# Last layer of a four-layer convolution kernel: two 64-column matmuls side by side, two kinds of tap pairs, weights prepared ahead by GpSimd

## The chip, the core and the metric

The kernel runs on one core of one Trainium2 chip. Its metric is device time in microseconds (us), the median over the timed executions. A core has a matmul engine (TensorE, "PE", whose weight loads are listed as "PEld"), VectorE ("DVE"), ScalarE ("ACT"), GpSimd ("POOL") and SyncE ("SP"), which here only issues DMAs. Each engine has an instruction stream of its own; they meet at semaphores.

## The reference, cut to what matters

Four layers are applied to `x` of 2 x 128 channels x 128 x 128 in float32: an attention along columns, four directional scans, a deformable convolution, and the layer that is changed. Before each stands a group normalisation.

```python
x = x + _L3_conv_ref(_gn(x), L3_conv_weight, L3_conv_bias)

def _L3_conv_ref(x, weight, bias):      # KERNEL 4, STRIDE 2, padding 1
    patches = _extract_patches(x)       # b c h w p q: 64 x 64 patches of 4 x 4
    hmt1 = jnp.einsum('up,bchwpq,qv->bchwuv', _H, patches, _H)
    hmt2 = jnp.einsum('pu,bchwpq,qv->bchwuv', _H2, patches, _H2)
    m1 = jnp.einsum('bchwuv,ocuv->bohwuv', hmt1, weight[:half])
    m2 = jnp.einsum('bchwuv,ocuv->bohwuv', hmt2, weight[half:])
    o1 = jnp.einsum('au,bohwuv,cv->bohwac', _IH, m1, _IH)
    o2 = jnp.einsum('au,bohwuv,cv->bohwac', _IH2, m2, _IH2)
    hmult = jnp.concatenate([o1, o2], axis=1)
    ...
    return out + bias
```

`_H` and `_H2` hold only 1 and -1, `_IH` and `_IH2` only 1/4 and -1/4. Each patch gives a 2 x 2 block of outputs; the lower 64 output planes use one set of matrices, the upper 64 another. The scan layer before it matters for one reason: a row of it is a 9-tap convolution of the finished row before, so 4 x 127 steps follow one another strictly.

## The kernel before, in words

The image stays in SBUF as `res` (128 channels on the partitions). `layer0_prepare`, `layer0_attention`, `Merge.run`, `layer1` (the scans), `layer2` and `layer3` run one after the other. A helper, `InOrder`, keeps the instructions of an engine in the order of the Python program; all of them show under line 81.

`layer3` (line 1652) works in 32 blocks: for each of two images, 16 blocks of `RB = 8` rows, which are 4 x 64 patches. Per block:

- `normalise` (ACT, two activations of 128 x 640) writes the normalised even and odd columns, with a rim of zeros that GpSimd sets, to `col0` and `col1`.
- `transform` (DVE, eight `tensor_tensor` of 128 x 640) makes four planes `x` from sums and differences of neighbouring columns: the transform along a row is done, that down the column is not.
- `multiply` (PE) does 32 matmuls, each with 128 x 128 weights out of `weff` and 256 moving columns: for each of the four planes and both output rows, four taps summed in PSUM. One float32 matmul is two instructions in the trace, with a weight load each.
- `finish` (ACT two, DVE eight operations) combines the four planes, adds the bias and the residual `res`, and SP stores the block.

`multiply` of block i stands ahead of `finish` of block i-1 and `transform` of block i+1, and all tiles but one are double. The weights `weff` are made between the layers: `w3` (1 MB) is loaded once layer 2 is over, DVE makes sums and differences of it (lines 1673 and 1674), and DVE and ACT scale 32 pieces each (lines 1682 and 1686).

`layer1` (line 1039) starts with a group norm, loads the weights of three scans on ACT's DMA queue (`wl`, line 1033), lets GpSimd add taps (`ws`, line 1035), and normalises four rows on ACT before the first step of the scan:

```python
        ahead = 4
        for h in range(ahead):
            normalise(h)
```

`load_columns` fetches tiles `x1t` that only the fourth scan reads; three of these loads are issued at the start of the layer.

Three other places of the kernel use matmuls with fewer than 128 output columns, which lie side by side on PSUM's partitions: `ps_off` (line 1234, layer 2, four outputs of 32), and in `layer0_prepare` `ps_m` and `pg` (two of 64).

Of the kernel before, what the change touches and what calls it, by code (L numbers as in the profile page):

```python
# [7 lines left out]
F32 = mybir.dt.float32  # L8
I32 = mybir.dt.int32
AF = mybir.ActivationFunctionType  # L10
ALU = mybir.AluOpType
# [5 lines left out]
N = 2  # L17
# [1011 lines left out]
def scan_weights(env, prm, pool, d):  # L1029

    nc = env.nc
    wl = pool.tile([P, 9, P], F32, name=f"wl{d}", tag=f"wl{d}")
    nc.scalar.dma_start(out=wl, in_=prm["wscan"][:, d])
    ws = pool.tile([P, 4, P], F32, name=f"ws{d}", tag=f"ws{d}")
    nc.gpsimd.tensor_tensor(ws, wl[:, 2:9:2, :], wl[:, 1:8:2, :], ALU.add)
    return wl, ws


def layer1(env, prm, res, both, x1_d, st_gn, st_next, first):

# [3 lines left out]
    with ExitStack() as ctx:  # L1046
# [3 lines left out]
            gs, gb = env.group_norm(cp, pn, st_gn, "l1")  # L1050
        pp = ctx.enter_context(tc.tile_pool(name="l1ps", bufs=2, space=PSUM))
        weights = [first] + [scan_weights(env, prm, cp, d) for d in range(1, 4)]


        lines = [
# [10 lines left out]
        CB = 8  # L1066

        def load_columns(w0):
            t = sp.tile([P, N, CB, S], F32, name="x1t", tag="x1t")
            nc.sync.dma_start(out=t, in_=x1_d[:, :, w0 : w0 + CB, :])  # L1070
            return t

# [576 lines left out]

def layer3(env, prm, res, st_gn, out):

    nc, tc = env.nc, env.tc
    flip = (1, 0, 2, 3)
    RB = 8
    with ExitStack() as ctx:  # L1660
        cp = ctx.enter_context(tc.tile_pool(name="l3c", bufs=1))
        bias = cp.tile([P, 1], F32, name="bias3", tag="bias3")
        nc.scalar.dma_start(out=bias, in_=prm["b3"])
        weff = cp.tile([P, 4, 2, 4, P], F32, name="weff", tag="weff")
        with tc.tile_pool(name="l3w", bufs=1) as wp:
            ta = wp.tile([P, 16 * P], F32, name="ta", tag="ta")
            tb = wp.tile([P, 16 * P], F32, name="tb", tag="tb")
            nc.scalar.dma_start(out=ta, in_=prm["w3"])
            a, b = ta, tb
            for bit in range(2):  # L1670
                va = a.rearrange("p (h t k) -> p h t k", t=2, k=P << bit)
                vb = b.rearrange("p (h t k) -> p h t k", t=2, k=P << bit)
                nc.vector.tensor_tensor(vb[:, :, 0], va[:, :, 0], va[:, :, 1], ALU.add)
                nc.vector.tensor_tensor(vb[:, :, 1], va[:, :, 0], va[:, :, 1], ALU.subtract)
                a, b = b, a
            what = a.rearrange("p (u v o) -> p u v o", u=4, v=4)
            for u in range(4):
                for c in range(2):
                    for q in range(4):
                        to = weff[:, u, c, q, :]  # L1680
                        sign = (1, -1, 1, -1)[u]
                        nc.vector.tensor_scalar(
                            to[:, 0:64], what[:, u, (c + 1) ^ q, 0:64], sign / 16, None, ALU.mult
                        )
                        sign = (-1, 1, 1, -1)[u] * (-1, 1)[c]
                        nc.scalar.mul(  # L1686
                            to[:, 64:128],
                            what[:, (0, 3, 2, 1)[u], (3, 2)[c] ^ flip[q], 64:128],
                            sign / 16,
                        )  # L1690

        sp = ctx.enter_context(tc.tile_pool(name="l3s", bufs=2))
        with tc.tile_pool(name="l3pn", bufs=1, space=PSUM) as pn:
            gs, gb = env.group_norm(cp, pn, st_gn, "l3")
        pp = ctx.enter_context(tc.tile_pool(name="l3ps", bufs=2, space=PSUM))
        pe, dve, act = (InOrder(tc, e) for e in (nc.tensor, nc.vector, nc.scalar))
        blocks = [(n, h) for n in range(N) for h in range(0, S, RB)]

        def normalise(i):

            n, h = blocks[i]
            lo, hi = max(0, h - 1), min(S, h + RB + 1)
            cols = [
                sp.tile([P, RB + 2, 65], F32, name=f"col{k}", tag=f"col{k}") for k in range(2)
            ]
            nc.gpsimd.memset(cols[0][:, :, 0:1], 0.0)  # L1706
            nc.gpsimd.memset(cols[1][:, :, 64:65], 0.0)  # L1707
            for k in range(2):
                if h == 0:
                    nc.gpsimd.memset(cols[k][:, 0, :], 0.0)  # L1710
                if h == S - RB:
                    nc.gpsimd.memset(cols[k][:, RB + 1, :], 0.0)
            rows = slice(lo - h + 1, hi - h + 1)
            for k in range(2):
                act.activation(
                    cols[k][:, rows, 1 - k : 65 - k],
                    res[n][:, lo:hi, 1 - k :: 2],
                    AF.Identity,
                    bias=gb[:, n : n + 1],
                    scale=gs[:, n : n + 1],  # L1720
                )
            return cols

        def transform(cols):

            x = sp.tile([P, 4, RB + 2, 64], F32, name="x3", tag="x3")
            t = sp.tile([P, 2, RB + 2, 64], F32, name="t3", tag="t3", bufs=1)
            for k, op in ((0, ALU.add), (2, ALU.subtract)):
                even, odd = x[:, k], t[:, k // 2]
                dve.tensor_tensor(even, cols[0][:, :, 0:64], cols[0][:, :, 1:65], op)  # L1730
                dve.tensor_tensor(odd, cols[1][:, :, 0:64], cols[1][:, :, 1:65], op)
                dve.tensor_tensor(x[:, k + 1], even, odd, ALU.subtract)
                dve.tensor_tensor(even, even, odd, ALU.add)
            return x

        def multiply(x):
            got = []
            for u in range(4):
                ps = pp.tile([P, 2, RB // 2, 64], F32, name=f"m{u}", tag=f"m{u}")
                for c in range(2):  # L1740
                    for q in range(4):
                        pe.matmul(
                            ps[:, c],
                            lhsT=weff[:, u, c, q, :],
                            rhs=x[:, u, q : q + RB - 1 : 2, :],
                            start=(q == 0),
                            stop=(q == 3),
                        )
                got.append(ps.rearrange("p c h w -> p (c h w)"))
            return got  # L1750

        def finish(i, m):

            n, h = blocks[i]
            t = sp.tile([P, 512], F32, name="t", tag="t")
            s = sp.tile([P, 512], F32, name="s", tag="s")
            act.activation(t, m[3], AF.Identity, bias=bias)
            act.copy(s, m[2])
            for half, k in ((slice(0, 64), (0, 1)), (slice(64, 128), (1, 0))):
                dve.tensor_tensor(t[half], m[k[0]][half], t[half], ALU.add)  # L1760
                dve.tensor_tensor(s[half], m[k[1]][half], s[half], ALU.add)
            ot = sp.tile([P, RB, S], F32, name="ot", tag="ot")
            o = ot.rearrange("p (h a) (w c) -> p a c h w", a=2, c=2)
            r = res[n][:, h : h + RB, :].rearrange("p (h a) (w c) -> p a c h w", a=2, c=2)
            tv = t.rearrange("p (c h w) -> p c h w", c=2, w=64)
            sv = s.rearrange("p (c h w) -> p c h w", c=2, w=64)
            for a, op in enumerate((ALU.add, ALU.subtract)):
                dve.tensor_tensor(o[:, a], tv, sv, op)
                dve.tensor_tensor(o[:, a], o[:, a], r[:, a], ALU.add)
            nc.sync.dma_start(out=out[n, :, h : h + RB, :], in_=ot)  # L1770

        count = len(blocks)
        cols = {0: normalise(0), 1: normalise(1)}
        xs = {0: transform(cols.pop(0))}
        ms = {}
        for i in range(count + 1):
            if i < count:
                ms[i] = multiply(xs.pop(i))
            if i >= 1:
                finish(i - 1, ms.pop(i - 1))  # L1780
            if i + 2 < count:
                cols[i + 2] = normalise(i + 2)
            if i + 1 < count:
                xs[i + 1] = transform(cols.pop(i + 1))

# [3 lines left out]
def program(ctx, tc, prm, out):  # L1791
# [12 lines left out]
        "sv": dram.tile([P, N, NC, WC, S], F32, name="sv_d", tag="sv_d"),  # L1804
        "sve": dram.tile([P, N, NC, S, WC], F32, name="sve_d", tag="sve_d"),
    }
    x1_d = dram.tile([P, N, S, S], F32, name="x1_d", tag="x1_d")
    mem["px"] = dram.tile([N, TP, TP, P], F32, name="px_d", tag="px_d")
    mem["off"] = dram.tile([N, NT, P, 4, 27], F32, name="off_d", tag="off_d")
# [14 lines left out]
    with tc.tile_pool(name="l1w", bufs=1) as wp:  # L1824
        first = scan_weights(env, prm, wp, 0)
        merge.run(prm, res, mv, st_gn[1])
        merging.close()
        layer1(env, prm, res, both, x1_d, st_gn[1], st_gn[0], first)
    layer2(env, prm, res, mem, tables, st_gn[0], st_gn[1])
    layer3(env, prm, res, st_gn[1], out)  # L1830


def constants(np):
# [126 lines left out]
```

## Time and profile before

| | us |
|---|---|
| median of 3 runs | 5750.13 (5746.08 to 5760.94) |
| the profiled execution | 5755.18 |
| its span, first to last instruction | 5753.0 |
| layer 3's matmuls, first to last | 5298.2 to 5742.6 |
| PE busy in the span | 5381.7 |

The span is cut by time: layer 0's preparation up to about 460, the attention to about 1985, the merge to 2169, the scans to about 3810, layer 2 to 5280, layer 3 from there. In a group's line, the number after the bar is the time in which at least one instruction of the group ran; then the mean length of one, which for matmuls contains the way through the array and so is longer than their spacing.

### The profile page before, as it was taken

The numbers are of one execution on the slowest core, as the hardware profiler recorded it, in microseconds if no ns is written. First come the engines' busy times: TensorE is split into PE (matmuls) and PEld (weight loads), VectorE is DVE, ScalarE is ACT, GpSimd is POOL, SyncE is SP. The second block draws the span as 40 slices with busy tenths as digits, with TensorE's granted clock in tenths as the row PEclk, the third lists the DMA queues.
The fourth block names the chain that finished last, engine by engine and source line by source line (L and its number), as shares of the span: only waits on it lengthen the run. The fifth ranks groups of instructions, "written<-read, shape, count | busy, mean of one in ns | idle before, by whom it ended". The sixth has DMA issues, their size and how long they took to land. (4 is left out here: it accounts for less than half of the span.)

```text
span 5753.0 us, 162512 instructions
## 1 busy us (share of the span) xinstructions
PE 5381.7 (94%) x67323; PEld 4838.1 (84%) x67323; DVE 3775.1 (66%) x7289; ACT 2647.0 (46%) x7928; POOL 1288.8 (22%) x983
## 2 busy tenths in 40 slices
PE   8997999999999708999999999997999999998999
PEld 8866888888888608999999999963999999998888
DVE  3645888888888765555555566643666666666887
ACT  1046989898888774442223320022333333333221
POOL 2113666666666530000000013310000000000000
PEclk9998999999999859999999999998999999999999
DMA  3243333333333491000000001125766677663001
GB/s 146 96 189 105 62 62 60 59 62 62 59 59 58 125 373 50 2 1 1 1 1 1 1 16 39 44 65 118 87 88 88 87 84 90 88 87 50 41 37 41
DMA packets 413668, 401.01 MB, mean 70 GB/s; under 512 B 63488, under 2 KB 368512, under 8 KB 402304
## 3 DMA queue, kind: packets, MB, share of 16 engines
q1 hardware_dynamic: 403856, 363.87, 30.9%
q10 hardware_dynamic: 9072, 26.64, 1.2%
q8 instruction: 541, 8.86, 0.7%
q14 instruction: 199, 1.63, 0.1%
HBM read 251.00 MB, written 139.37 MB: 68 GB/s over the span
## 5 line engine op out<-in xcount | busy, mean ns | idle before, releaser
L81 PE MATMUL pl<-ln,wl 128*128 128x128 f32 (+1 forms) x10160 | 1240.7, 276 | 7.4 <-DVE ln L81 7.2
L81 PEld LDWEIGHTS pl<-ln,wl 128*128 128x128 f32 x10160 | 1176.2, 190 | 18.3 <-DVE ln L81 4.4
L81 ACT ACTIVATE e<-e,mx 128x128 f32<-128x128 f32 x2048 | 793.4, 395 | 0.8 <-DVE mx L81 0.8
L81 ACT COPY sm<-ps_s 128x432 f32<-128x432 f32 (+1 forms) x768 | 318.3, 487 | 803.3 <-PE ps_s L81 803.3
L81 ACT COPY res<-ln 128x128 f32<-128x128 f32 x762 | 262.0, 344 | 720.4 <-DVE ln L81 720.4
L81 POOL TENSOR_TENSOR e<-e,total 128x1024 f32<-128x1024 f32 x256 | 485.9, 1898 | 478.1 <-DVE total L81 470.3
L81 DVE COPY s<-ps_w 100x1152 f32<-100x1152 f32 x256 | 346.5, 1354 | 307.1 <-PE ps_w L81 307.1
L81 PE MATMUL ps_s<-s,xw 100*128 100x144 f32 x4096 | 545.1, 286 | 0.2 <-ACT sm L81 0.2
L81 PE MATMUL po<-sm,wdef 128*128 128x256 f32 x2304 | 539.1, 379 | 0.0
L81 PE MATMUL pl<-ln,ws 128*128 128x128 f32 x4064 | 536.8, 273 | 0.0
L81 POOL COPY et<-et 128x1024 f32<-128x1024 f32 x256 | 516.1, 2016 | 35.7 <-DVE et L81 27.0
L81 PEld LDWEIGHTS ps_s<-s,xw 100*128 100x128 f32 x4096 | 517.1, 190 | 0.7 <-ACT sm L81 0.7
L81 DVE TENSOR_TENSOR v<-pl,c 128x128 f32<-128x128 f32 x508 | 148.2, 292 | 538.0 <-PE pl L81 538.0
L81 PEld LDWEIGHTS pl<-ln,ws 128*128 128x128 f32 x4064 | 494.5, 190 | 0.0
L81 ACT ACTIVATE r<-gen,alphas 128x1536 f32<-128x1536 f32 x256 | 394.9, 1543 | 174.2 <-PE gen L81 145.3
L81 POOL TENSOR_TENSOR res<-ln,x1t 128x128 f32<-128x128 f32 x256 | 134.4, 525 | 1485.1 <-DVE ln L81 1485.1
L81 PEld LDWEIGHTS po<-sm,wdef 128*128 128x128 f32 x2304 | 419.8, 190 | 47.6
L81 PE MATMUL m<-x,weff 128*128 128x256 f32 x2048 | 444.4, 380 | 14.8 <-DVE x L81 14.8
L81 PEld LDWEIGHTS m<-x,weff 128*128 128x128 f32 x2048 | 390.6, 191 | 68.3 <-issue 14.9
L1706 POOL MEMSET col<- 128x10 f32 x32 | 3.7, 116 | 1869.1 <-ACT weff L1686 1490.7
L81 ACT ACTIVATION_READ_ACCUMULATOR e<-e,mx 128x1 f32 x2048 | 396.7, 194 | 0.0
L81 DVE SCALAR_TENSOR_TENSOR ln<-v,res 128x128 f32<-128x128 f32 x1016 | 343.7, 338 | 49.2 <-DVE v L81 1.3
(225 smaller groups left out, 8806.6 us busy)
## 6 DMA issues: line engine op xcount, KB each, us to landing
xw<-px_d SPq DMA_DIRECT2D x1280, 80.0 KB
xa<-in_x SPq DMA_DIRECT2D x16, 1024.0 KB
v_d<-vs SPq DMA_DIRECT2D x16, 1024.0 KB
qb_d<-sb SPq DMA_DIRECT2D x16, 1024.0 KB
qa_d<-sa SPq DMA_DIRECT2D x8, 2048.0 KB
zz<-qb_d SPq DMA_DIRECT2D x1024, 16.0 KB
vt<-v_d SPq DMA_DIRECT2D x64, 256.0 KB
qk<-qa_d SPq DMA_DIRECT2D x256, 64.0 KB
```

Source lines behind the costliest of these rows:

```text
L81: return lambda *a, **k: self.tc.keep_in_program_order(issue(*a, **k))
L1706: nc.gpsimd.memset(cols[0][:, :, 0:1], 0.0)
```

## The change

The 2 x 2 outputs of a patch are sums and differences of PSUM results; the change takes another factoring. Outputs' lower 64 planes ("half 0") and upper 64 ("half 1") now get their own moving operands, so a matmul has 64 output columns, and the two of a pair write partitions 0 to 63 and 64 to 127 of the same PSUM tile `m3`. A block has 48 such matmuls (32 for `m3`'s second half, 16 for its first), hence 96 instructions with float32's two passes, where 64 with 128 columns stood before. Half 0's operands come from pairs of taps across columns (`first`, DVE: `dm`, `dp`, then four `q`), half 1's from pairs across columns and rows (`second`, GpSimd: `ap`, `am`, two `b`). `normalise` writes the odd columns a second time, to a PSUM tile `odd3` (`again`). `combine` (ACT one, DVE four operations) makes the output, and GpSimd adds the residual in `finish`. Tiles `col0`, `col1`, `am`, `dp`, `odd3` are single, `dm`, `ap`, `b`, `ot` double, `q` sixfold, `m3` threefold. The factor 1/16 goes into the group norm's scale.

The weights are made by GpSimd in `layer3_weights`, called at the start of `layer1`: load `ta`, 25 additions and subtractions of 128 x 256, store as `w3_d` (1.3 MB) to DRAM. `layer3` loads them again on SP's queue. `x1t` moves to a pool of its own, opened after that. In the instruction order of the changed kernel, ACT's stream at this place reads: load `wl` of the last scan, load `ta`, store `w3_d` with a wait for GpSimd, the first normalised rows of the scan. GpSimd's reads: a memset, three `ws`, the 25 operations, and nothing more until the fourth scan.

```diff
 def layer1(...):
         weights = [first] + [scan_weights(env, prm, cp, d) for d in range(1, 4)]
+        prepare()
+        xp = ctx.enter_context(tc.tile_pool(name="l1x", bufs=3))
...
-            t = sp.tile([P, N, CB, S], F32, name="x1t", tag="x1t")
+            t = xp.tile([P, N, CB, S], F32, name="x1t", tag="x1t")
...
+def layer3_weights(env, prm, w3_d):
...
+        nc.scalar.dma_start(out=ta.rearrange("p u v o -> p (u v o)"), in_=prm["w3"])
+        pool = nc.gpsimd
...
+                    pool.tensor_tensor(to, ta[:, :, x, part], ta[:, :, y, part], op)
...
+        nc.scalar.dma_start(out=w3_d, in_=w3)
...
 def layer3(...):
-        weff = cp.tile([P, 4, 2, 4, P], F32, name="weff", tag="weff")
...
+        w3 = cp.tile([P, W3], F32, name="w3", tag="w3")
+        nc.sync.dma_start(out=w3, in_=w3_d)
...
+            for t in (gs, gb):
+                nc.vector.tensor_scalar(t, t, 1.0 / 16, None, ALU.mult)
...
+            again = pp.tile([P, 1024], F32, name="odd3", tag="odd3")
+            again = again[:, 0 : (RB + 2) * 65].rearrange("p (h w) -> p h w", w=65)
+            act.copy(again, cols[1])
...
+        def second(cols):
+            even, odd = cols
...
+            pool.tensor_tensor(ap, even, odd, ALU.add)
+            pool.tensor_tensor(am, even, odd, ALU.subtract)
+            for k, op in enumerate((ALU.subtract, ALU.add)):
+                pool.tensor_tensor(b[:, k], am[:, 0::2, :], am[:, 1::2, :], op)
...
+        def first(cols, again):
...
+            for to, op in ((dm, ALU.subtract), (dp, ALU.add)):
+                dve.tensor_tensor(to[:, 0], again[:, :, 0:H], even[:, :, 1:65], op)
+                dve.tensor_tensor(to[:, 1], even[:, :, 0:H], again[:, :, 1:65], op)
+            for k in range(4):
+                q = sp.tile([P, 2, RH, H], F32, name="q3", tag="q3", bufs=6)
...
+                dve.tensor_tensor(q, dp[:, :, lo : lo + RB - 1 : 2, :],
+                    dp[:, :, hi : hi + RB - 1 : 2, :], ...)
...
-            for u in range(4):
-                for c in range(2):
-                    for q in range(4):
-                        pe.matmul(ps[:, c], lhsT=weff[:, u, c, q, :],
-                            rhs=x[:, u, q : q + RB - 1 : 2, :], ...)
+            parts = ((0, one), (1, two))
+            for c in range(2):
+                for q in range(4):
+                    for y in range(2):
+                        for half, part in parts:
+                            if half == 0:
+                                rhs = dm[:, y, q : q + RB - 1 : 2, :]
+                            else:
+                                rhs = ap[:, q : q + RB - 1 : 2, y : y + H]
+                            pe.matmul(ps[part, 1, c], lhsT=rows_weight(half, c, q, y), rhs=rhs, ...)
+            for r in range(2):
+                for x in range(2):
+                    for y in range(2):
+                        for half, part in parts:
...
+                            pe.matmul(ps[part, 0, r], lhsT=ws[:, 2 * r + x, y, part], rhs=rhs, ...)
...
+        def combine(ps):
+            act.activation(c, ps[:, 0, 0], AF.Identity, bias=bias)
...
+                dve.tensor_tensor(g[:, k], c, ps[:, 0, 1], op)
...
+                dve.tensor_tensor(o[:, k], g, ps[:, 1], op)
...
+            pool.tensor_tensor(ot, ot, res[n][:, h : h + RB, :], ALU.add)
             nc.sync.dma_start(out=out[n, :, h : h + RB, :], in_=ot)
...
+        for i in range(-1, count + 2):
+            if i in planes:
+                ms[i] = multiply(*planes.pop(i))
+            if i + 1 < count:
+                planes[i + 1] = second(there[0]) + first(*there)
+            if i - 2 in ots:
+                finish(i - 2, ots.pop(i - 2))
+            if i - 1 in ms:
+                ots[i - 1] = combine(ms.pop(i - 1))
+            if i + 2 < count:
+                there = normalise(i + 2)
```

## The prediction, made before the changed kernel was run

> **What bounds the kernel now.** I read the page first, then the busy time in stretches, then the timeline where the change touches it.
>
> ```profile
> span 5753.0 us, 162512 instructions
> PE 5381.7 (94%) x67323; PEld 4838.1 (84%) x67323; DVE 3775.1 (66%) x7289; ACT 2647.0 (46%) x7928; POOL 1288.8 (22%) x983
> ...
> L81 PE MATMUL m<-x,weff 128*128 128x256 f32 x2048 | 444.4, 380 | 14.8 <-DVE x L81 14.8
> ```
>
> PE is busy nearly everywhere, but that is an average over stages. The stretches of the last layer (us, then busy time and instructions by engine, granted clock, DMA):
>
> ```profile
> core 0: us, PE busy (x) PEld busy (x) DVE busy (x) ACT busy (x) POOL busy (x), PEclk, DMA share, GB/s
> ...
> 5280.00:5298.00 18.00, 0.56 (x2) 0.50 (x2) 14.80 (x52) 9.72 (x38) 0.42 (x6) 0.56 0.17 59
> 5298.00:5745.00 447.00, 444.42 (x2048) 390.58 (x2048) 361.28 (x503) 89.15 (x124) 7.91 (x66) 0.99 0.09 37
> ```
>
> In the 444 us of matmuls PE never rests, DVE has 361 us, GpSimd almost nothing. So this stretch is PE's: one block per 13.815 us (ACT's first read of a finished block is at 5314.42, that of the last at 5742.68, 31 blocks later), 64 instructions at 215.9 ns. Before it PE stands for 18 us while weights are made and the first planes formed. After the last matmul (5742.6) 10.4 us of combining and storing follow.
>
> The second place is the scan's start, where the weights' preparation is put (start, length, engine, instruction):
>
> ```profile
> 2169.11 0.82 ACTq L1033 DMA_DIRECT2D wl<-in_wscan  x2
> ...
> 2173.28 1.26 POOL L1035 TENSOR_TENSOR ws<-wl 128x512 f32<-128x512 f32 x1 [11.26 <-DVE gs_l L44]
> 2173.32 0.20 ACT L45 ACTIVATE gs_l<-gs_l 128x2 f32<-128x2 f32 x1 [6.96 <-DVE gs_l L44]
> 2173.33 0.34 ACTq L1033 DMA_DIRECT2D wl<-in_wscan  x1
> ...
> 2174.59 4.72 ACT L81 ACTIVATE res<-res,gb_l,gs_l 128x128 f32<-128x128 f32 x12 [1.07 <-DVE gb_l L69]
> ```
>
> The third `wl` load waits for nothing of its own, yet is issued 4 us after the other two, behind the activation that waited for DVE: ACT's DMA issues and activations are one line. The scan's first matmul is at 2175.88, right after the first rows of `res`; from there everything is serial, so a delay of these rows is a delay of the end.
>
> **Part 1, the matmuls.** 96 instructions take the place of 64. Alone each would take the same 216 ns (256 columns; fewer weight columns do not shorten the moving stream), so all hangs on whether the two halves run at once. The trace has two such groups:
>
> ```profile
> 384.10 1.09 PE L81 MATMUL pg<-zt 128*64 128x65 f32 x30
> ...
> 3829.47 3.62 PE L1234 MATMUL ps_off<-gx,woff 128*32 128x512 f32 x32
> ```
>
> `pg` has two neighbours of 64 columns: single starts are 384.208, 384.215, 384.267, 384.273, so two every 58.5 ns. 65 columns alone would take 65 x 215.9/256 = 55 ns each: a pair costs one plus 3.5 ns. `ps_off` starts four of 512 every 428 ns, where one alone takes 432. So a pair of 256 is 216 to 219; I take 217. Per block 48 x 217 = 10.42 us, times 32 = 333.3, against 32 x 13.815 = 442.1: **-108.8 us**. Each half reads its own moving tile in `pg` and `ps_off` too.
>
> Against this stands the Trainium skill, "TensorE: Matmul & The Clock Gate", section "Measured speedup vs the span model": three column tiles gave 2.38 times, not 3. At that efficiency (0.79) a pair would take 216 x 2/1.59 = 272 ns, a block 13.05 us, and the gain would be 25 us, about what part 3 takes back. That figure is for single packs with their way through the array; here packs follow one another as in `ps_off`, which measured 3.98 of 4 in steady state. The trace decides.
>
> **Part 2, does anything else need over 10.42 us a block?** DVE: `dm`, `dp` four at 0.82 (row `x<-col`, 818 ns), `q` four at 0.69 (512 elements as `ot<-t,s`, 689), `g` two at 0.42 (256 elements with PSUM as `vs<-ps_zb`, 415), `o` two at 0.69: 8.26 us, less than the 12 of before. ACT: two normalisations 0.93, the copy to PSUM, not in the trace (between the 0.49 of `sm` at 432 elements and 0.97; I take 0.75), bias 0.45: 3.1 us. GpSimd is new here. Its rows for two different inputs (`acc`: 130 elements 467 ns, 260 elements 738) give 0.2 us + 2.08 ns per element: `ap`, `am` 1.55 each, `b` 0.88 twice, `ot` 2.33, two memsets 0.12: 7.4 us. Planes for block i+1 are made while block i multiplies, and most inputs have two buffers, so each queue only has to keep the period.
>
> DVE and GpSimd can stop one another. In the merge:
>
> ```profile
> 2123.76 1.23 DVE L81 TENSOR_TENSOR res<-te,res 128x1024 f32<-128x1024 f32 x1
> 2123.81 3.42 POOL L81 TENSOR_TENSOR res<-te,res 128x1024 f32<-128x1024 f32 x1 [5.25 <-DVE te L81]
> ```
>
> Shortest, median and longest of the same kinds, by tile:
>
> ```profile
> L81 POOL TENSOR_TENSOR e<-e,total x256: 1896/1898/1902, 505.2 to 1979.4; 128x1024 f32<-128x1024 f32 x128
> ...
> L81 POOL TENSOR_TENSOR res<-te,res x16: 2359/3422/3447, 2012.6 to 2158.6; 128x1024 f32<-128x1024 f32 x16
> ```
>
> GpSimd's addition takes 2.36 us without company and 3.42 when it starts inside DVE's: it waits for DVE's end (2124.99), then runs 2.24. In the attention, with DVE at work all the time on operands of which at most one is in SBUF, 256 additions stay within 6 ns of each other. This is what the skill states ("SBUF — State Buffer", section "Who interferes with whom"): a DVE instruction with two SBUF inputs and a GpSimd instruction that reads SBUF exclude one another; with one it does not. `dm`, `dp`, `g`, `o` have one input in PSUM, so only the `q` exclude. By the rule: GpSimd 7.2 + `q` 2.76 = 9.9 us of exclusive time per block, still under 10.42; if every DVE instruction excluded, 7.2 + 8.26 = 15.4, over 13.8. I take the first: no cost. The cover is thin: 0.5 us on the shared entrance, 2.2 on DVE.
>
> **Head and tail of layer 3.** The weights come by DMA (1.3 MB; `ta`'s 1 MB took 4.4 us from 5280.69), before the scales are ready: without the weight operations between them, DVE's chain ends near 5285.2 (5284.6, then 0.15 for `gb` and 0.17 twice for the factor). Normalise 2 x 0.86, copy 0.75, `dm` 0.82: the first matmul at about 5289.0 instead of 5298.2: **-9.2**. `b` and `q` have the 6.9 us of the row matmuls for cover. Both starts pay about 2.2 us of half clock (granted 0.5 until 5302.55). Tail: 0.2 + bias 0.45 + 0.1 + `g` 0.84 + `o` 1.38 + 0.1 + `ot` 2.33 + issue and landing as before 4.2 = 9.6 instead of 10.4: **-0.8**.
>
> **Part 3, the weights at the scan's start.** ACT now has to load `ta` and issue the store of `w3_d` before the first normalised row, and that store waits for GpSimd's 25 operations. Queued behind it: the 12 activations, then DVE's copies, PE's first row, all of the scan. GpSimd: `ta` is issued near 2173.7, behind the third `wl` (0.59 MB). Before, that `wl` landed at 2182.2 because three `x1t` loads (3 MB) were in front; these now wait for the preparation's memory, so `ta` lands earlier: 4.4 us for itself plus 1.4 for `wl`, about 2179.5 (bounds 2177.5 and 2182). The three `ws` (1.27) fit before. Then 25 x 0.73 (256 elements between the rows of 130 and 260; lower bound 0.65 from `L183`, 1.75 ns per element, upper 0.78) = 18.4: 2197.9, issue 0.6, first row at 2198.6 instead of 2174.59: **+24.0** (18 to 29). Nothing hides it, PE has been idle for 173 us there. GpSimd's operations themselves would be free beside the scan; the wait in ACT's line is what costs. The store's bytes and the later `x1t` loads delay nobody: `x1t` is read 1200 us later. SP gets one more issue, at the layer's start, ahead of stores that come 20 us later.
>
> **Sum.** -108.8 - 9.2 - 0.8 + 24.0 = -94.8 on the profiled execution's 5755.2: 5660.4. The median of the runs is 5.05 below that execution, so 5655.
>
> **The rivals.**
> (a) The shared entrance or DVE sets the period. If GpSimd runs at its slow rows (2160 elements in 4780 ns: `ap` 1.63, `b` 0.92, `ot` 2.46) exclusive time is 10.3, and with DVE's in-order queue held at each `q` a period of 11.2 is likely: +25, 5680; at worst (each `q` behind a GpSimd instruction) 11.7, 5697. For it: two queues in strict order. Against: GpSimd's wait overlaps 0.12 of its own start.
> (b) ACT does not stand behind the store (it is handed over and waits elsewhere): +24 goes, 5631. Against: the third `wl`.
> (c) Slower than before: the pairs do not overlap, 96 x 215.9 = 20.73 us a block, +221 - 10 + 24: 5985. The turning point is a pair of 279 ns (32 x 48 x pair = 442.1 + 10 - 24). For it: another pattern than `pg`'s, with 256 columns and weights that change with each instruction. Against: `pg` and `ps_off`. At the skill's packing figure it would end at 5739, not told apart from no change.
>
> **How the numbers follow.** 0.65 for the forecast, 0.19 for (a), 0.09 for (b), 0.03 for (c), 0.01 for the packing in between, 0.03 for slower otherwise or much faster. A measurement here tells about 0.3% (17 us) from no change; all cases but (c), the packing figure and 0.01 of the rest lie beyond that on the fast side: faster 0.95, same 0.01, slower 0.04. The range: part 3's bounds (-6, +5) and a pair at 216 to 219 (-2, +3) give 5647 to 5664 alone; taking in (a) and most of (b), 5634 to 5697.
>
> **What would show it.** Right: `m3`'s matmuls 3072 in about 335 us, starting two together; DVE idle before `dm` or `g`, not PE before `m3`; the first `res` activation near 2198 with a GpSimd release; scan steps as long as before. Wrong: PE idle before `m3` with `q` or `b` as releaser (a); the first row at 2175 (b); 660 us of `m3` (c).

## The result, and the profile after

The changed kernel takes 5645.36 us (median of 4 runs, 5644.19 to 5656.64), the kernel before beside it 5748.1 us (4 runs, 5744.51 to 5760.94). The ratio is 0.9822, with a 95% interval of 0.9802 to 0.9842: 1.8% faster. The forecast was 5655, ten microseconds above. The profiled execution took 5645.21 us, with a span of 5643.4.

From the page of the kernel after, the span and the busy time by engine:

```profile
span 5643.4 us, 164496 instructions
PE 5270.7 (93%) x68347; PEld 4712.5 (84%) x68347; DVE 3697.0 (66%) x7127; ACT 2648.5 (47%) x7896; POOL 1549.2 (27%) x1169
```

There are 1024 more matmul instructions, and PE is still busy 93% of the time: the page alone does not tell what happened. The stretches do (the head of the last layer, then its matmuls; us, then busy time and instructions by engine, granted clock, DMA share, GB/s):

```profile
core 0: us, PE busy (x) PEld busy (x) DVE busy (x) ACT busy (x) POOL busy (x), PEclk, DMA share, GB/s
5280.00:5298.30 18.30, 9.68 (x52) 8.41 (x50) 5.84 (x17) 5.84 (x10) 1.91 (x5) 0.83 0.21 72
5298.30:5634.40 336.10, 335.99 (x3072) 264.45 (x3072) 295.63 (x379) 94.80 (x124) 245.94 (x227) 0.99 0.13 50
```

The last layer's matmuls took 444.42 us for 2048 instructions; now 3072 take 335.99. PE is busy throughout; GpSimd has gone from 8 to 246 us in this stretch, and DVE from 361 to 296. The groups of matmuls, with the idle time of PE before each in the last column, say that nothing was waited for:

```profile
L81 PE MATMUL m<-ap,w 128*64 128x256 f32 x1021 | 229.0, 381 | 0.0
L81 PE MATMUL m<-dm,w 128*64 128x256 f32 x1021 | 228.1, 382 | 0.0
L81 PE MATMUL m<-q,w 128*64 128x256 f32 x512 | 116.1, 380 | 0.0
L81 PE MATMUL m<-b,w 128*64 128x256 f32 x512 | 115.9, 378 | 0.0
```

The busy times of the four groups add up to 689 us in 336: two ran at any time. (The 380 ns are the recorded length of one, from entering to leaving the array; one enters every 216.) The starts of the first `dm` matmul of each block are 12.35 us apart at first, then ten times 10.36, then 10.43 and 10.44 in turn: 215.8 and 217.4 ns for each of 48 pairs.

The other place is the scan's start (start, length, engine, line, instruction, idle time before it and releaser):

```profile
2167.21 0.20 ACT L45 ACTIVATE gs_l<-gs_l 128x2 f32<-128x2 f32 x1 [6.96 <-DVE gs_l L44]
2167.22 0.33 ACTq L1033 DMA_DIRECT2D wl<-in_wscan  x1
2167.89 0.33 ACTq L1681 DMA_DIRECT2D ta<-in_w  x1
...
2174.07 4.81 POOL L1703 TENSOR_TENSOR tb<-ta 128x256 f32<-128x256 f32 x7 [1.48 <-DMA ta<-in_w]
...
2191.29 0.33 ACTq L1720 DMA_DIRECT2D w_d<-w3w  x1
2191.67 4.72 ACT L81 ACTIVATE res<-res,gb_l,gs_l 128x128 f32<-128x128 f32 x12 [24.25 <-POOL w3w L1692]
```

ACT stands for 24.25 us between the scales and the first normalised row, and what released it is GpSimd's last operation on `w3w`, by way of the store that is issued 0.4 us ahead of the row. Before, the row came 1.27 us after the activation of the scales (2173.32 to 2174.59); now 24.46 us after it (2167.21 to 2191.67).

### The profile page after: what moved, and what is told of

Same layout as the page of the kernel before. It is cut to its first block, busy times and chain, and to the rows that moved or that the text cites. A ratio compares the mean times of both kernels' runs of the same rounds, so it can differ in the third digit from the quotient of the medians.

```text
span 5643.4 us, 164496 instructions
## 1 busy us (share of the span) xinstructions
PE 5270.7 (93%) x68347; PEld 4712.5 (84%) x68347; DVE 3697.0 (66%) x7127; ACT 2648.5 (47%) x7896; POOL 1549.2 (27%) x1169
## 5 line engine op out<-in xcount | busy, mean ns | idle before, releaser
L81 PE MATMUL te<-cst_main,e 128*128 128x128 f32 x2048 | 338.5, 288 | 24.5 <-POOL e L81 17.3
L81 DVE COPY et<-te 128x512 f32<-128x512 f32 x512 | 348.1, 680 | 11.5 <-PE te L81 10.9
```

What stands on the lines that cost most here:

```text
L81: return lambda *a, **k: self.tc.keep_in_program_order(issue(*a, **k))
```

## The experiments

Theory: the gain is the pairs of matmuls (108 us) and the shorter head (10 us); all that is paid is ACT's line, held by the store. Rivals: the preparation costs something else; PE's pairing hangs on the order of the instructions or doesn't; DVE and GpSimd are near to being the bound. The kernel before took 5745 us beside the first four runs, 5764 beside the next four and 5754 beside the last two, so what is compared below is mostly stages of the profiles, which repeat far better than whole times. Experiments 4 to 10 are one execution each.

**1. The store issued by SyncE.**

```diff
-        nc.scalar.dma_start(out=w3_d, in_=w3)
+        nc.sync.dma_start(out=w3_d, in_=w3)
```

> The changed kernel with one word changed: the store of w3_d is issued by SyncE instead of ScalarE. Theory (ScalarE's line, held by a store that waits for GpSimd's 25 operations, is all that the preparation costs): the 24.25 us of idle time before the first normalised row go, that row starts within 2 us of the end of the merge's scales, and the kernel runs about 23 us less than the changed kernel's 5645, so near 5622; ratio to the kernel before about 0.978. Rival 1 (GpSimd's work beside the scan costs as well: it excludes VectorE and delays the scan's first steps, or its memory does): 5 to 20 of the 23 us come back as longer first scan steps, 5627 to 5642. Rival 2 (the first row waits for something else of the new part, the load of ta or the third wl): no change, 5645. The loads of x1t, now queued on SyncE behind the store, are read 1200 us later and should cost nothing under any theory.

Measured: 5626.44 us (median of 5), ratio to the kernel before 0.98 (0.9786 to 0.9814); the changed kernel run beside it 5649.34 (median of 4), its ratio to the kernel before 0.9837 (0.9822 to 0.9852). So 22.9 us faster than the changed kernel. The profile at the scan's start:

```profile
2170.80 0.20 ACT L45 ACTIVATE gs_l<-gs_l 128x2 f32<-128x2 f32 x1 [8.05 <-DVE gs_l L44]
2172.11 4.72 ACT L81 ACTIVATE res<-res,gb_l,gs_l 128x128 f32<-128x128 f32 x12 [1.10 <-DVE gb_l L69]
...
2190.49 0.72 POOL L1692 TENSOR_TENSOR tk<-zero,tk 128x256 f32<-128x256 f32 x1
2190.57 0.79 DVE L81 SCALAR_TENSOR_TENSOR ln<-v,res 128x128 f32<-128x128 f32 x1
2191.18 0.77 POOL L1716 TENSOR_TENSOR w3w<-tk 128x256 f32<-128x256 f32 x1
```

The row comes 1.31 us after the scales, as before the change, and GpSimd now prepares the weights while the scan runs. The last three lines are the small remainder of rival 1: DVE's `ln<-v,res`, two inputs in SBUF, starts inside GpSimd's operation and takes 0.79 us instead of its usual 0.29, and GpSimd's next one starts only near its end. Added over the steps beside the preparation this is 2.9 us, and the scan's first pass is 404.0 us long instead of 401.0. The theory holds; the sum from the profile is 23.2 won and 3 paid, 20.2 net, where the medians differ by 22.9 and the runs of the two spread over 16 and 11 us. This is the fastest version of the study.

**2. The preparation alone, with the last layer of before.** The diff to the kernel before is the changed `layer1` and `layer3_weights`; `layer3` stays, and the stored weights are read by nobody.

> The last layer is that of the kernel before (it makes its own weights again), and only the preparation and its store on ScalarE are put in at the scan's start; the stored weights are read by nobody. Theory: the scan's first row comes 23 to 24 us later and all else is as before, so 5748 + 23 = about 5771, ratio 1.004. Rival (the preparation's 24 us are partly won back behind it, as the changed kernel's shorter second layer start suggests, because the program up to the last layer is the same here): second layer's start is 7 us shorter than in the kernel before, about 5764. If the 13 us that the changed kernel gained outside the scan's start and the last layer are only the spread between executions, this profile and the copy of the kernel before show merge ends anywhere from 2153 to 2160 us and layer 2 starts (end of the offsets' matmuls to the first ps_w) anywhere from 35 to 40 us, in no order.

Measured: 5770.22 us against 5744.93, ratio 1.0042 (1.0027 to 1.0058): 25 us slower, on the expected 23. The wait is the same:

```profile
2195.72 4.72 ACT L81 ACTIVATE res<-res,gb_l,gs_l 128x128 f32<-128x128 f32 x12 [24.06 <-POOL w3w L1692]
```

From the scales to the row it is 24.26 us, then matmuls of 444.32 us as in the kernel before. Nothing is won back behind it.

**3 and 4. Both kernels once more.** The changed kernel's first profile was 13.7 us faster than the change accounts for (below). No edit.

> The changed kernel once more, for the spread of its stages between executions: 5645 within 6 us. Theory of spread: the stages up to the scan, and from the last scan step to the first ps_w, differ from the first profile by some us; what the change reaches does not: 3072 matmuls of the last layer in 336.0 us within 0.5, 8.1 us ahead of them, 9.0 behind, 24.2 us of idle time before the first normalised row. Rival (those stages are changed by the change): they repeat within 1 us.

> The kernel before once more, one execution: 5748 within 8 us. Theory of spread: the merge's end and the second layer's start differ from the first profile by up to 7 us while the scan's four passes and the last layer (444.4 us of matmuls) repeat within 1 us. Rival: they repeat within 1 us, and the changed kernel's 13 us there belong to the change.

Measured, by stage, in us (M: end of the merge's last `res` on DVE; G: from the last offsets' matmul of layer 2 to its first `ps_w`; S: from the scales to the scan's first row; H: from the group norm that follows layer 2, at DVE's first `mv_l`, to the last layer's first matmul; L: its matmuls; T: from the last matmul to the end of the span):

| kernel | M | G | S | H | L | T |
|---|---|---|---|---|---|---|
| before, first profile | 2159.8 | 39.4 | 1.27 | 17.74 | 444.42 | 10.45 |
| before_again | 2158.0 | 34.2 | 1.30 | 17.77 | 444.61 | 10.45 |
| preparation_only | 2157.9 | 40.7 | 24.26 | 17.75 | 444.32 | 10.03 |
| changed, first profile | 2153.7 | 35.1 | 24.46 | 8.10 | 335.99 | 9.04 |
| changed_again | 2153.9 | 34.5 | 24.49 | 8.10 | 335.65 | 9.04 |
| store_on_sync | 2156.2 | 34.3 | 1.30 | 7.89 | 336.77 | 9.04 |

S, H, L and T repeat within 0.5 us where the same code runs (but L of store_on_sync is 0.8 to 1.1 us above the other two). G took 39.4 us in one profile of the kernel before and 34.2 in the other (34.2 to 40.7 over the twelve profiles of this study), and M lies anywhere between 2148.4 and 2159.8 in the twelve. The two changed profiles repeated M within 0.2 us, as the rival said, but the later runs, the same up to there in all but the last layer, had 2152.7, 2155.7, 2149.3, 2156.7, 2148.4 and 2157.9. So of the 13.7 us, 10.4 lie in two stages that vary like this from one profile to the next (6.1 in M, 4.3 in G), and the first profile of the kernel before had both near their long end; the rest lies in small differences of the stages between, 1.6 us of it in layer 2's offsets. What makes the two stages vary the runs don't show. The medians of the runs made here side by side, 5744.93 (9 runs) and 5649.34 (4), differ by 95.6 us, within 1 us of the sum of the steps (96.3, below).

**5 and 6. How far apart may the two halves stand?** Each call of `pe.matmul` is two instructions (3072 instructions are 48 calls for each of 32 blocks), so even the changed kernel issues A A B B. The two runs put two calls of a half together, and then a whole accumulation group (8 calls of the columns' part, 4 of the rest).

```diff
-                    for y in range(2):
-                        for half, part in parts:
+                    for half, part in parts:
+                        for y in range(2):
```

```diff
-                for q in range(4):
-                    for y in range(2):
-                        for half, part in parts:
+                for half, part in parts:
+                    for q in range(4):
+                        for y in range(2):
```

(and the same for the loops of `qs` and `b`.)

> The changed kernel with two loops of the matmuls exchanged: two calls of one half (four instructions, since each call of fp32 is two) stand before two calls of the other, instead of one and one. Same 96 instructions per block, same data. Theory (PE starts instructions in order; one starts when its own columns are free and its predecessor has started): A A A A B B B B takes 6 slots for 8 instructions instead of 4, since only the last of a run has the first of the next beside it; 72 slots of 216 ns, 15.55 us per block instead of 10.42, last layer +164 us, 5809. Rival (the two column halves have queues of their own, or look several instructions ahead): no change, 10.42 us per block, 5645.

> The changed kernel with the half as the outer loop of each accumulation group: runs of 16 and of 8 instructions of one half. Theory of order as in the run before: 30 slots for 32 instructions and 14 for 16, so 88 slots, 19.0 us per block, +275 us, 5920; this is also what the change would have cost with the same matmuls in the plain order, slower than the kernel before. Rival (queues of their own): 10.42 us per block, or somewhere between if they look a few instructions ahead.

Measured: in pairs of calls 5647.38 us, matmuls 336.1: no change. By group 5776.14, matmuls 461.5, 14.32 us per block. The strict order, on which my expectation rested, is refuted by the first run, and full independence by the second. The timeline of the second, at the boundary of two runs of 16 instructions, shows what is there instead (consecutive instructions of one kind come as one line with their number):

```profile
5463.57 0.43 PE L81 MATMUL m<-dm,w 128*64 128x256 f32 x1
...
5464.27 2.32 PE L81 MATMUL m<-dm,w 128*64 128x256 f32 x10
5466.22 0.43 PE L81 MATMUL m<-ap,w 128*64 128x256 f32 x1
```

`dm`'s run of 16 begins at 5463.57, beside the last four `b` of the run before. The line of ten is its 4th to its 13th instruction, one every 216 ns; the 5th to the 12th go alone. The 13th starts at 5466.214, and the first `ap` enters 6 ns later. So the last four of a run have company, and no others. It is the same for runs of 8: they begin 0.92 us apart, which is four slots of 216 ns and 0.055. Four runs of 16 at 12 slots (2.65 us) and four of 8 at 4 slots make 14.3 us per block, as measured.

**7. Runs of eight instructions throughout.** This tests that reading on a number not yet seen.

```diff
-                for q in range(4):
-                    for y in range(2):
-                        for half, part in parts:
+                for q2 in range(2):
+                    for half, part in parts:
+                        for q, y in ((2 * q2 + j // 2, j % 2) for j in range(4)):
```

(and the half outermost in the loops of `qs` and `b`, which have four calls each.)

> The changed kernel with four calls of one half (eight instructions) before four of the other. In the run halves_by_group the next run's first instruction started beside the 13th of 16 and the 5th of 8, 0.055 us after it: the last four of a run had company, whatever its length. Theory (PE has at most four instructions waiting or running per column half before its queue stops): a run of eight takes 4 slots of 216 ns and 0.055 us, 12 runs per block are 12 x 0.919 = 11.03 us instead of 10.42, matmuls 336 + 19 = 355 us, about 5665. Rival 1 (strict order, only the neighbour): 7 slots per run, 18.1 us per block. Rival 2 (what slowed halves_by_group was something else than the length of its runs, such as the last group's late planes): 10.42 us per block.

Measured: 5673.44 us, matmuls 357.27, 11.08 us per block in every block, against 11.03 expected, 18.1 by strict order and 10.42 if the length of the runs did not matter. The reading holds: the other half's run enters when four instructions of the current run are left, the one just starting among them. The layer's start tells whether four instructions count or the 0.86 us that four of them take. Until 5308.68 the granted clock was 0.5 in this run, and an instruction entered every 427 ns:

```profile
5305.34 2.37 PE L81 MATMUL m<-dm,w 128*64 128x256 f32 x5 [5.16 <-DVE dm L81]
5307.07 0.69 PE L81 MATMUL m<-ap,w 128*64 128x256 f32 x1
```

The first `ap` again enters beside the fifth of eight, with 1.7 us of `dm` left. So it is the number of instructions; another size of matmul wasn't run.

**8. The odd columns left in SBUF.** This takes away the third part of the change, the copy in PSUM.

```diff
-            again = pp.tile([P, 1024], F32, name="odd3", tag="odd3")
-            again = again[:, 0 : (RB + 2) * 65].rearrange("p (h w) -> p h w", w=65)
-            act.copy(again, cols[1])
-            return cols, again
+            return cols, cols[1]
```

> The changed kernel without the copy of the odd columns to PSUM: the four dm and dp operations of VectorE read two tiles in SBUF. ScalarE has one copy of 0.7 us per block less; VectorE's work is the same in number and size. Theory (two SBUF inputs on VectorE and GpSimd exclude one another): exclusive time per block is GpSimd's 6.9, q 2.8 and dm, dp 3.3, so 13.0 us at least against PE's 10.42, with the strict order of both queues 13 to 14.5: last layer +83 to +131 us, 5728 to 5776, and PE idle before m. Rival (exclusion not of weight; the copy does nothing): 10.42 us per block, 5645.

Measured: 5678.27 us; matmuls 372.3 us, so +36.3; 11.78 us per block in steady state. PE and DVE in that profile, by groups:

```profile
L81 PE MATMUL m<-dm,w 128*64 128x256 f32 x998 | 227.8, 382 | 24.1 <-DVE dm L81 24.1
...
L81 DVE TENSOR_TENSOR dp<-col,col 128x640 f32<-128x640 f32 x62 | 129.1, 2121 | 0.0
...
L81 DVE TENSOR_TENSOR dm<-col,col 128x640 f32<-128x640 f32 x62 | 96.8, 1599 | 0.0
```

With `odd` in PSUM `dm` and `dp` take 0.81 us each, in every block; the tile's line of the changed kernel (shortest, median and longest in ns):

```profile
L81 DVE TENSOR_TENSOR dm<-odd,col x32: 810/816/825, 5297.5 to 5616.2; 128x640 f32<-128x640 f32 x32
```

With both inputs in SBUF and GpSimd at work they take 1.60 and 2.12 on average, though DVE does the same work (the kernel before has the same shape from two SBUF inputs, `x<-col`, at 0.82 without GpSimd), and PE waits for them. So the copy is worth 36 us and costs ACT 0.7 us per block that nobody waits for. The size was off: I had expected at least 13.0 us per block, the sum of the 13 operations that exclude one another. In steady state one of them is under way in 99% of the time, but the time from the end of one to the end of the next is 0.03 to 0.16 us less than the length that the next has alone (only for the first `q` it is 0.1 us more). Over the 13 this makes the 1.2 us of difference.

**9 and 10. The same cover, tried from GpSimd's side.** First one more subtraction per block, then, as a control, three memsets of the same tile, which take longer but read nothing.

```diff
             pool.tensor_tensor(am, even, odd, ALU.subtract)
+            pool.tensor_tensor(am, even, odd, ALU.subtract)
```

```diff
+            for _ in range(3):
+                pool.memset(am, 0.0)
             pool.tensor_tensor(am, even, odd, ALU.subtract)
```

> The changed kernel with GpSimd's am computed twice per block (1.56 us more, the same values). GpSimd's own work is then 8.5 us per block, under PE's 10.42. Theory of exclusion: 8.5 + q 2.8 = 11.3 us exclusive, more than 10.42, so PE begins to wait: 11.3 to 12.6 us per block, last layer +28 to +70 us, 5673 to 5715. Rival (each engine counts by itself): hidden, 10.42 us per block, 5645.

> The changed kernel with three memsets of am (650 elements each) in GpSimd's queue where the run one_more_on_gpsimd had one more subtraction. From the rows of memsets (10 elements 0.12 us, 256 elements 0.31) a memset of 650 should take about 0.6 us: 1.9 us per block, no less than the subtraction's 1.56, but it reads nothing. Theory (what cost 11.9 us there is the exclusion between VectorE's q, dm or dp with two SBUF inputs and GpSimd instructions that read SBUF): a memset excludes nobody, so the last layer stays at 336 us of matmuls, 5645. Rival (GpSimd's queue as such is too long, or its results come too late for PE): the matmuls take 348 us or more, as with the subtraction.

Measured: with the subtraction 5665.75 us, matmuls 347.87 (+11.9), blocks of 10.36, 11.87 and 10.71 in turn, 10.98 on average in steady state. With the memsets 5639.6 us, matmuls 335.63: nothing. One line of PE of the first and two of the second, the last a line of the second's timeline:

```profile
L81 PE MATMUL m<-dm,w 128*64 128x256 f32 x1024 | 230.6, 382 | 13.7 <-DVE dm L81 13.2
```

```profile
L81 PE MATMUL m<-dm,w 128*64 128x256 f32 x1001 | 222.4, 380 | 0.0
```

```profile
5449.59 2.04 POOL L81 MEMSET am<- 128x650 f32 x3
```

1.56 us more of GpSimd's reading per block costs PE 8.6 us of waiting between its matmuls (the other 5.2 of the 13.7 stand before the layer's first matmul, as in the changed kernel; a wait is counted only as far as it outlasts the recorded 380 ns of the matmul before it, and so the 11.9 are more than 8.6). 2.04 us more of writing costs none. It is the exclusion, then, and not the length of GpSimd's queue. In the second run 29 `q` start inside a memset and take 0.68 us each; the 31 that start inside `ap` take 1.80 to 2.10, the 29 inside `ot` 1.31 to 2.53. That is what the Trainium skill states ("SBUF — State Buffer", section "Who interferes with whom"): a DVE instruction with two SBUF inputs contends with a GpSimd instruction that reads SBUF, "not with one that only writes it".

## Why the prediction was right, step by step

| step | predicted | in the profiles |
|---|---|---|
| matmuls of the last layer | -108.8 | -108.4 (444.42 to 335.99) |
| head of the last layer | -9.2 | -9.6 (17.74 to 8.10) |
| tail | -0.8 | -1.4 (10.45 to 9.04) |
| preparation at the scan's start | +24.0 | +23.2 (1.27 to 24.46) |
| sum | -94.8 | -96.3 |
| outside the change | 0 | -13.7 (spread) |
| profiled execution against profiled execution | -94.8 | -110.0 (5755.2 to 5645.2) |

**Matmuls: right.** A pair costs 215.8 to 217.4 ns against my 217, read from `pg` and `ps_off`. My "3.98 of 4" for `ps_off` does not come out of its starts: four enter every 429 to 431 ns, where one of 512 columns alone would take 432 by the estimate, so it is all 4. The Trainium skill's figure for a pack of three ("TensorE: Matmul & The Clock Gate", "Measured speedup vs the span model"), by which as an estimate a pair would take 272 ns and the kernel about 5739, does not describe packs that follow one another: here two give 2.0 of 2. Three side by side were not run. The start at half clock (granted 0.5 until 5302.37) cost 1.9 us (the first block took 12.35 us), near the 2.2 that I had put on both sides.

What I had not seen is a condition of it. The trace of before could not show how far apart the partners may stand. With the halves as outer loops, which is how one would write it first, the same matmuls would have taken 461.5 us, more than the 444.4 of the kernel before (experiment 6).

**No cost on DVE and GpSimd: right, and experiments 8 to 10 show the exclusion behind it.** The single durations: `ap` 1.56 us without company (predicted 1.55), `b` 0.76 (0.88), `ot` 2.37 (2.33), `q` 0.69 (0.69), the copy 0.70 (0.75). Rival (a) needed the slow end of these and did not come. DVE and GpSimd do hold one another up: `q` has a median of 0.69 but a mean of 1.14 and a maximum of 2.06, `am` a median of 2.02. But PE's idle time between the matmuls is 0. I had the cover too thin: experiment 9 adds 1.56 us and lengthens the block by 0.57 (10.41 to 10.98), so about 1.0 us was free, not 0.5. Adding up durations overstates exclusive time: 11.3 by the sum, 10.98 measured; in experiment 8 13.0 and 11.78. `q` ends 0.55 us after the recorded end of an addition it stood behind, though alone it takes 0.68; this overlap, at 13 operations a block, is the 1.2 us of experiment 8. The cover is better reckoned from the ends of such operations than from their lengths.

**Head and tail: right.** `col`, the copy and `dm` came as costed (1.69, 0.70, 0.82), and the weights were there in time. The tail's steps came 0.6 us shorter in all.

**ACT's line: right, with errors that largely cancel.** `ta` became usable 6.9 us after the scales, not 6.2; GpSimd's operations are 0.73 long, as predicted, but begin every 0.68, since each starts before its predecessor's record ends, so 25 took 17.2 us, not 18.4 (25 x 0.73 is 18.3 in any case). From the last of them to the row it was 0.4 us, not 0.7. The three leave the delay 0.8 us shorter than forecast. Rival (b), that ACT isn't held, is excluded by the wait in the profile and by experiment 1: moving that one store to SyncE gave 22.9 us back.

**The rest.** The forecast of 5655 is 10 us above the measured median of 5645. The profiled execution of before, against whose time the sum was made, had both of its variable stages near their long end; the correction of 5.05 us to the median of the runs took up part of that. How near the whole time came to the forecast is therefore in part chance. The sum of the steps, off by 1.5 us, owes to chance only what cancelled in ACT's line. Against the second profile of the kernel before (5746.5) the changed kernel's is 101.3 us shorter, 5 more than the sum of its steps, and 4.4 of these are the end of the merge. A sum over steps can be good to 2 us where two single executions differ by 10 for reasons of their own.

## What to carry to other kernels

When a buffer is prepared by one engine and stored by DMA, look at which engine's line issues the store and what stands behind it: here one word, the queue of a store that nobody needs for 3000 us, was worth 23 us. Two matmuls with half the columns each cost one, if they alternate closely in program order; write the half as the innermost loop. An operand moved to PSUM by an idle engine can free two engines that exclude one another in SBUF; before filling an idle GpSimd, count what it reads against DVE's instructions with two SBUF inputs, and not against DVE's busy time.

## What the runs showed of the hardware that was not expected

- PE finds a partner for a matmul within a short distance only: runs of one half of 2 and of 4 instructions cost nothing (10.41 and 10.42 us per block), runs of 8 gave 11.08 and of 16 and 8 mixed 14.32. In the last two, the next run's first instruction enters when four of the current run are left, counting the one that enters then (in the runs of 8 at a granted clock of 0.5 as at 1.0). It thus starts ahead of three instructions that stand before it in the program.
- GpSimd's memset of 650 elements takes 0.64 us, and neither it (0.63 to 0.66) nor a DVE `q` with two SBUF inputs that starts inside it (0.68, 29 times) gets longer; the same tile's subtraction takes 1.56, and in the changed kernel the 15 `q` that start inside it take 2.05.
- An execution's spread has its places: 34 to 41 us from the offsets to the first `ps_w`, and 11 us in the end of the merge over twelve profiles, where the stages that the change touches repeat within 0.5 us for the same code, but for one of 1.1.
